# Mamba scan: two channel blocks in one scan of 1024 columns, parted by a factor of zero, with the carried state of the second block added by ScalarE

## The chip, the core and the metric

The kernel runs on one core of a Trainium2 chip. The metric is the device time of one execution in microseconds (us). Five engines have instruction queues of their own and run beside each other: TensorE (PE, with its weight loads shown as PEld), VectorE (DVE), ScalarE (ACT), GpSimd (POOL) and SyncE (SP, which only issues transfers here). Each takes its instructions in the order in which they were put into its queue; an instruction that waits holds up all that stand behind it on the same engine.

## The reference, cut to what matters

A network of four layers is computed: a Mamba layer, a dynamic convolution, linear attention with a mixture of experts, and softmax attention with a second mixture of experts. The change touches only the Mamba layer. It has two blocks (m1, m2), each over 2 images of 1024 tokens, with 512 channels and 16 states per channel:

```python
delta = softplus(dt @ dt_w + dt_b)
A = -exp(A_log)
dA = exp(delta[..., None] * A)                       # decay, per token, channel and state
dBu = delta[..., None] * Bm[:, :, None, :] * xs[..., None]
def step(hst, ins):
    dA_t, dBu_t, C_t = ins
    hst = dA_t * hst + dBu_t                         # the recurrence over tokens
    y_t = einsum('bdn,bn->bd', hst, C_t)             # sum over the 16 states
    return (hst, y_t)
h0 = zeros((b, D_INNER, D_STATE))
_, ys = scan(step, h0, ...)
y = (ys + xs * Dp) * silu(res)
```

The recurrence runs over tokens; channels and states are independent of one another. A new image starts from zero.

## The kernel before, in words

**Units.** The 2 x 1024 tokens are cut into four chunks of 512 (`TC`). A unit is one chunk of one block: m1 chunks 0 to 3, then m2 chunks 0 to 3, eight units one after the other. Chunks 0 and 2 start an image (`first`, state zero); chunks 1 and 3 take over the state that the chunk before left in `state`.

**Layout.** The 512 channels lie as four blocks (`dc`) of 128 partitions, the 512 tokens along the columns. `scan(j, ...)` loops over the 16 states `n`. For one state it does this:

1. GpSimd (L461) makes two tiles `h` of 128x1024, each for two channel blocks (`G = 2`): `du * B`. There are six buffers, three states' worth.
2. ScalarE (L468) makes for each channel block a tile `da = exp(delta * A)` of 128x512 in PSUM, out of a pool of three banks.
3. VectorE (L472) runs for each channel block a `tensor_tensor_scan` of 512 columns, `h = da * h(previous column) + h`, in place. In a first chunk it starts at 0.0; otherwise at a [128, 1] column of `state`.
4. TensorE (L440) turns `h` in `rest(n, hs)`: for each of four groups of 128 tokens four transposes, one for each channel block, fill one bank of the pool `ht` (three banks). VectorE (L449) then does `ya += ht * C`, one 128x512 instruction for each bank. For states 0 and 10 ScalarE (L447) writes the bank into `ya` or `yb` in place of that.
5. In a first chunk `keep` (L432) has ScalarE copy the last column of `h` into `state`.

**What else runs.** While a unit is scanned, the front of the next unit (projection, causal convolution, SiLU, softplus) and the back of the one before (gate, output projection, norm) are interleaved: `between` hands out their steps, `before` hands out the steps of `rest`, and both are called after each scan. These steps put matmuls into TensorE's queue, activations and table loads into ScalarE's, and elementwise work into GpSimd's. A scheduler then settles the order on each engine with costs of its own; the names of the tiles and their buffer counts decide what an instruction has to wait for. So a buffer count can move instructions that the diff does not touch.

**PSUM in this layer.** Eight banks: `m_mm` 2 (fronts, backs), `m_ht` 3, `m_da` 3. In the last unit the `m_da` pool is closed and replaced by 2 banks plus 1 bank in which the first part of the next layer's convolution is already summed up (L762).

The core of the loop before:

```python
for dc in range(NDC):
    da = self.ps_da.tile([P, TC], F32, tag="da", ...)
    nc.scalar.activation(da, delta[:, dc, :], AF.Exp, scale=self.aneg[:, i : i + 1])
    h = hs[dc // G][:, dc % G, :]
    nc.vector.tensor_tensor_scan(
        h, da, h, 0.0 if first else state[:, n, dc : dc + 1], ALU.mult, ALU.add)
    next(before, None)
    if n or dc:
        next(between, None)
```

Of the kernel before, what the change touches and what calls it, by code (L numbers as in the profile page):

```python
# [10 lines left out]
F32 = mybir.dt.float32  # L11
I32 = mybir.dt.int32
BF16 = mybir.dt.bfloat16
AF = mybir.ActivationFunctionType
ALU = mybir.AluOpType
AX = mybir.AxisListType
PSUM = bass.MemoryType.PSUM
DRAM = bass.MemoryType.DRAM

P = 128  # L20
# [7 lines left out]
TC = 512  # L28
# [3 lines left out]
NDC = DI // P  # L32
NS = 16
# [200 lines left out]
class Mamba:  # L234
# [7 lines left out]
    def __init__(self, net, m, pools, xt, x, in_w, out_w, xproj_w, dt_w):  # L242
        self.net, self.m, self.xt, self.x = net, m, xt, x
        self.wpool, self.one, self.two, self.scanp, self.dram, self.ps_mm, self.ps_da, self.ps_ht = pools
        self.weights = in_w, out_w, xproj_w, dt_w
        self.chunks = {}
        self.carry = None
# [45 lines left out]
    def front(self, j, alone=False):  # L293


        net, nc, m, one, two = self.net, self.net.nc, self.m, self.one, self.two
# [76 lines left out]
        delta = two.tile([P, NDC, TC], F32, tag="delta", name=f"{m}_delta_{j}")  # L373
# [3 lines left out]
        for dc in range(NDC):  # L377
            pool, tag = (self.ps_ht, "ht") if alone and dc else (self.ps_mm, "mm")
# [36 lines left out]
    def scan(self, j, before, between, start=False):  # L415
# [5 lines left out]
        net, nc, m, scanp = self.net, self.net.nc, self.m, self.scanp  # L421
        xs, bd, ct, delta, du = self.chunks[j]
# [4 lines left out]
        G = 2  # L427
        half = [P, G, TC]

# [25 lines left out]
        for n in range(NS):  # L455
# [9 lines left out]
            for dc in range(NDC):  # L465
                da = self.ps_da.tile([P, TC], F32, tag="da", name=f"{m}_da_{j}_{n}_{dc}")
                i = dc * NS + n
                nc.scalar.activation(  # L468
                    da, delta[:, dc, :], AF.Exp, scale=self.aneg[:, i : i + 1]
                )  # L470
                h = hs[dc // G][:, dc % G, :]
                nc.vector.tensor_tensor_scan(  # L472
                    h, da, h, 0.0 if first else state[:, n, dc : dc + 1], ALU.mult, ALU.add
                )


                next(before, None)
                if n or dc:
                    next(between, None)
# [95 lines left out]
def layer0(net, x, x_dram, m1, m2, load_image, taps, conv_dram, lg):  # L575
# [5 lines left out]
    with (  # L581
# [6 lines left out]
        tc.tile_pool(name="m_ht", bufs=3, space=PSUM) as ps_ht,  # L588
        ExitStack() as last,
    ):  # L590
        ps_da = last.enter_context(tc.tile_pool(name="m_da", bufs=3, space=PSUM))
        xt = x.rearrange("p c b t -> p c (b t)")
        pools = (wpool, one, two, scanp, dram, ps_mm, ps_da, ps_ht)
# [20 lines left out]
        for u, (m, j) in enumerate(units):  # L614
# [17 lines left out]
            else:  # L632
                last.close()
                m.ps_da = last.enter_context(tc.tile_pool(name="m_da2", bufs=2, space=PSUM))
# [1108 lines left out]
```

## Time and profile before

| what | value |
|---|---|
| time, median of 3 runs (lowest to highest) | 2189.04 us (2184.31 to 2190.55) |
| span of the profiled execution | 2186.6 us |
| first and last scan of the Mamba layer start at | 53.3 us and 1030.1 us |
| share of the span busy: PE, DVE, ACT, POOL | 87%, 64%, 44%, 47% |
| scans: 256 from zero, 256 from a carried state | 303.3 us and 318.7 us of DVE |
| accumulates of L449 (448 of them) | 320.2 us of DVE |
| exponentials of L468 (512 of them) | 349.5 us of ACT |

The profile is that of one execution. Busy time of a group of instructions is a sum over records, and the records of neighbours on one engine can overlap by some tens of ns, so that the distance from start to start is the better price of an instruction where the engine never rests. "Idle before" is the time for which an engine stood still ahead of an instruction, with the instruction that released it. The first half of the span is the Mamba layer, the second half the other layers; the share of busy time over the whole span says little of either.

### The profile page before, as it was taken

Reading aid. Unit: us, or ns where it says so; the run is one execution under the profiler, and the core shown is the slowest. Engines: PE = TensorE matmul, PEld = TensorE weight load, DVE = VectorE, ACT = ScalarE, POOL = GpSimd, SP = SyncE. Lnnn points to the kernel's source line nnn. Section 1 sums busy time; section 2 is a strip of 40 time slices with the busy share of each in tenths; the row PEclk is TensorE's granted clock in tenths of the full one; section 3 lists DMA queues with packets and bytes.
Section 4 is the critical chain, followed back from the end, with each engine's and each line's share of the span. In section 5 each row is a group of like instructions: output and inputs, shape, how many; then the busy total and the mean of one; then the engine's idle time right before and its main releaser. Section 6 shows DMA issues by size and latency. Waiting matters only on the chain.

```text
span 2186.6 us, 27311 instructions
## 1 busy us (share of the span) xinstructions
PE 1894.0 (87%) x9652; PEld 1335.5 (61%) x9652; DVE 1400.3 (64%) x2210; ACT 959.2 (44%) x1610; POOL 1028.9 (47%) x726
## 2 busy tenths in 40 slices
PE   6888898898978888788999989949999599859996
PEld 2464555556555655454646556539999467649995
DVE  6999998999999999899005475752222544432223
ACT  4676677767777767645013454411111132301111
POOL 3796787959698686965025420012332000023331
PEclk9869889898989889899999999969999799979997
DMA  2121121111212111310030100028998200059997
GB/s 106 45 68 39 37 69 35 58 35 45 62 47 60 38 49 35 85 42 17 0 64 1 48 15 10 20 82 306 326 329 323 82 10 10 20 206 327 329 323 292
DMA packets 90499, 223.87 MB, mean 102 GB/s; under 512 B 35467, under 2 KB 51728, under 8 KB 79732
## 3 DMA queue, kind: packets, MB, share of 16 engines
q1 hardware_dynamic: 77636, 198.29, 27.1%
q0 software_dynamic: 7728, 19.15, 2.9%
q10 hardware_dynamic: 4992, 4.59, 0.7%
q8 instruction: 81, 1.33, 0.3%
q14 instruction: 62, 0.51, 0.1%
HBM read 204.60 MB, written 19.37 MB: 102 GB/s over the span
## 4 chain that ended last, share of the span: by engine, by line
PE 32%; DVE 22%; issue 19%; POOL 11%; ACT 10%; DMA 5%; POOLq 0%; SPq 0%; DVEq 0%; ACTq 0%
DVE m_h L472 11%; DVE m_ya L449 6%; PE acc L762 3%; POOL x L1520 3%; POOL l_yd L1570 3%; PE m_ht L440 3%; PE early_acc L762 3%; PE av L1276 3%; ACT m_da L468 2%; PE sc L1250 2%; DMA l_yd<-y,target 2%; POOL m_h L461 2%; PE h L1099 2%; PE m_xd_ps L351 1%; PE w L1108 1%
## 5 line engine op out<-in xcount | busy, mean ns | idle before, releaser
L461 POOL TENSOR_TENSOR m_h<-m_du,m_b 128x1024 f32<-128x1024 f32 x254 | 594.5, 2364 | 196.0 <-PE m_ht L440 95.8
L440 PE MATMUL m_ht<-ident,m_h 128*128 128x128 f32 x2048 | 361.2, 305 | 119.4 <-DVE m_ya L449 83.9
L440 PEld LDWEIGHTS m_ht<-ident,m_h 128*128 128x128 f32 x2048 | 259.5, 154 | 317.8 <-DVE m_ya L449 112.7
L468 ACT ACTIVATE m_da<-m_delta,m_aneg 128x512 f32<-128x512 f32 x512 | 349.5, 690 | 220.8 <-DVE m_h L472 220.1
L1520 POOL DMA_INDIRECT x<-l_zd,source x82 | 84.8, 1034 | 573.1 <-DVE source L1465 217.1
L449 DVE SCALAR_TENSOR_TENSOR m_ya<-m_ht,m_ct,m_ya 128x512 f32<-128x512 f32 x448 | 320.2, 733 | 18.4 <-PE m_ht L440 17.5
L472 DVE TENSOR_TENSOR_SCAN m_h<-m_da,m_state,m_h 128x512 f32<-128x512 f32 x256 | 318.7, 1271 | 14.7 <-POOL m_h L461 8.7
L472 DVE TENSOR_TENSOR_SCAN m_h<-m_da,m_h 128x512 f32<-128x512 f32 x256 | 303.3, 1210 | 23.6 <-ACT m_da L468 13.1
L1550 PEld LDWEIGHTS h<-xts,we 128*128 128x128 f32 x2528 | 298.4, 194 | 7.1 <-issue 3.4
L1550 PE MATMUL h<-xts,we 128*128 128x128 f32 x2528 | 299.4, 277 | 2.2 <-issue 1.7
L1557 DVE TENSOR_TENSOR hid<-hid,h 128x512 f32<-128x512 f32 x79 | 54.3, 688 | 258.9 <-PE h L1550 258.9
L1556 ACT ACTIVATE hid<-h 128x512 f32<-128x512 f32 x79 | 47.2, 598 | 384.6 <-issue 324.0
L1564 PE MATMUL o<-we,hid 128*128 128x256 f32 x632 | 150.4, 380 | 2.2 <-DVE y L1569 1.6
L1570 POOL DMA_INDIRECT l_yd<-y,target x79 | 79.3, 1003 | 142.6 <-DVE y L1569 136.3
L1564 PEld LDWEIGHTS o<-we,hid 128*128 128x128 f32 x632 | 113.7, 190 | 15.7 <-DVE y L1569 2.8
L336 PE MATMUL m_conv<-m_pre,m_taps 128*128 128x512 f32 x240 | 114.6, 596 | 6.7 <-ACT m_gate L498 5.6
L762 PE MATMUL early_acc<-x,early 128*98 128x448 f32 (+21 forms) x308 | 97.0, 447 | 0.0
L762 PE MATMUL acc<-x,pair 128*98 128x416 f32 (+21 forms) x308 | 93.6, 452 | 0.0
L1569 DVE COPY y<-o 128x256 f32<-128x256 f32 x79 | 33.6, 425 | 69.6 <-PE o L1564 69.6
L309 PE MATMUL m_in<-x,m_in_sb 128*128 128x512 f32 x128 | 68.8, 663 | 9.8 <-ACT m_pre L313 6.9
L762 PEld LDWEIGHTS acc<-x,pair 128*98 128x98 f32 x308 | 47.7, 167 | 39.9 <-issue 34.5
L528 PE MATMUL m_out<-m_out_sb,m_xs 128*128 128x256 f32 x256 | 68.7, 397 | 0.0
(318 smaller groups left out, 2843.3 us busy)
## 6 DMA issues: line engine op xcount, KB each, us to landing
we<-in_l_experts_dram SPq DMA_DIRECT2D x82, 1536.0 KB
m_b<-m_bd SPq DMA_DIRECT2D x128, 256.0 KB
w<-in_l_w_dram SPq DMA_DIRECT2D x21, 256.0 KB
l_zd<-l_z SPq DMA_DIRECT2D x7, 512.0 KB
l_yl<-l_yd SPq DMA_DIRECT2D x10, 256.0 KB
l_yl<-l_yd ACTq DMA_DIRECT2D x10, 256.0 KB
early<-taps SPq DMA_DIRECT2D x7, 343.0 KB
pair<-taps SPq DMA_DIRECT2D x7, 343.0 KB
```

What stands on the lines that cost most here:

```text
L309: nc.tensor.matmul(ps, lhsT=self.in_sb[:, kc, mc * P : (mc + 1) * P], rhs=self.xt[:, kc, tok], start=(kc == 0), stop=(kc == NCC - 1),)
L336: nc.tensor.matmul(ps, lhsT=self.taps[:, dc * 4 + k, :], rhs=pre[:, dc, k : k + TC], start=(k == 0), stop=(k == 3),)
L440: nc.tensor.transpose(ps[:, dc * P : (dc + 1) * P], hs[dc // G][:, dc % G, i * P : (i + 1) * P], net.ident,)
L449: nc.vector.scalar_tensor_tensor(ya[:, i, :], ps, c, ya[:, i, :], ALU.mult, ALU.add)
L461: (nc.vector if start and n == 0 else nc.gpsimd).tensor_mul(h, du[:, g * G : (g + 1) * G, :], b.unsqueeze(1).to_broadcast(half))
L468: nc.scalar.activation(da, delta[:, dc, :], AF.Exp, scale=self.aneg[:, i : i + 1])
L472: nc.vector.tensor_tensor_scan(h, da, h, 0.0 if first else state[:, n, dc : dc + 1], ALU.mult, ALU.add)
L762: nc.tensor.matmul(a[:, lo - 16 * k : hi - 16 * k, co : co + n], lhsT=lhsT, rhs=self.x[:, kc, b, lo - r0 : hi - r0, ci : ci + n], start=(u ...
L1520: nc.gpsimd.indirect_dma_start(out=x, out_offset=None, in_=zd[:, :], in_offset=bass.IndirectOffsetOnAxis(ap=source[:, g : g + 1], axis=0), ...
L1550: nc.tensor.matmul(ps[:, at], lhsT=w12[:, s, kc, at], rhs=xt[:, kc * P : (kc + 1) * P], start=(kc == 0), stop=(kc == NCC - 1),)
L1564: nc.tensor.matmul(ps[:, :C], lhsT=ht[:, mc * P : (mc + 1) * P], rhs=w[:, 8 + mc, :], start=(mc == 0), stop=(mc == NHC - 1),)
L1570: nc.gpsimd.indirect_dma_start(out=yd[g], out_offset=bass.IndirectOffsetOnAxis(ap=target[:, g : g + 1], axis=0), in_=y, in_offset=None, bo ...
```

## The change

Both channel blocks of a tile `h` are scanned by one instruction of 1024 columns. So that the second block does not take over the end of the first, its first decay factor is zero: column 0 of the second half of the factor tile is set to 0.0 once at the start and never written again, since the exponential of the second half now covers columns 1 to 511 only. Where a state is carried in, the first block still gets it as the scan's starting value; for the second block ScalarE adds `state * exp(delta[0] * A)` to the first column of `h` before the scan (one [128, 1] activation for each joined scan; the factors `a0` for all 16 states come from two small exponentials in each such unit). The purpose is fewer VectorE instructions with their fixed cost: 64 scans a unit become 32.

The factor tiles are two fixed tiles of two PSUM banks each, `das[0]` for channel blocks 0 and 1 and `das[1]` for 2 and 3. They take four banks in place of three, and the bank comes from `ht`, which goes from three to two. The last unit is not joined: its scans stay at 512 columns, with three banks of `da` in place of two, and `ht` at two. In the very first front one of the four `dt` products moves from the `ht` pool to the `mm` pool.

```diff
+        joined = self.das is not None
+        if joined and not first:
+            a0 = self.one.tile([P, NDC // G, NS], F32, tag="a0", name=f"{m}_a0_{j}")
+            for g in range(NDC // G):
+                dc = g * G + 1
+                nc.scalar.activation(
+                    a0[:, g, :], self.aneg[:, dc * NS : (dc + 1) * NS], AF.Exp,
+                    scale=delta[:, dc, 0:1],
+                )
...
-            for dc in range(NDC):
-                da = self.ps_da.tile([P, TC], F32, tag="da", name=f"{m}_da_{j}_{n}_{dc}")
-                i = dc * NS + n
-                nc.scalar.activation(
-                    da, delta[:, dc, :], AF.Exp, scale=self.aneg[:, i : i + 1]
-                )
-                h = hs[dc // G][:, dc % G, :]
-                nc.vector.tensor_tensor_scan(
-                    h, da, h, 0.0 if first else state[:, n, dc : dc + 1], ALU.mult, ALU.add
-                )
...
+            for g, h in enumerate(hs):
+                da = self.das[g] if joined else None
+                for q in range(G):
+                    dc = g * G + q
+                    i = dc * NS + n
+                    if joined:
+                        a, d = da[:, q, q:], delta[:, dc, q:]
+                    else:
+                        a = self.ps_da.tile([P, TC], F32, tag="da", name=f"{m}_da_{j}_{n}_{dc}")
+                        d = delta[:, dc, :]
+                    nc.scalar.activation(a, d, AF.Exp, scale=self.aneg[:, i : i + 1])
+                    if joined and q and not first:
+                        nc.scalar.activation(
+                            h[:, q, 0:1], state[:, n, dc : dc + 1], AF.Identity,
+                            scale=a0[:, g, n : n + 1], bias=h[:, q, 0:1],
+                        )
+                    if joined and q == 0:
+                        continue
+                    dc = g * G if joined else dc
+                    hq = h.rearrange("p g t -> p (g t)") if joined else h[:, q, :]
+                    nc.vector.tensor_tensor_scan(
+                        hq, da.rearrange("p g t -> p (g t)") if joined else a, hq,
+                        0.0 if first else state[:, n, dc : dc + 1], ALU.mult, ALU.add,
+                    )
+                    for _ in range(G if joined else 1):
+                        next(before, None)
+                        if n or dc:
+                            next(between, None)
+                        dc += 1
...
-        tc.tile_pool(name="m_ht", bufs=3, space=PSUM) as ps_ht,
+        tc.tile_pool(name="m_ht", bufs=2, space=PSUM) as ps_ht,
...
-        ps_da = last.enter_context(tc.tile_pool(name="m_da", bufs=3, space=PSUM))
+        ps_da = last.enter_context(tc.tile_pool(name="m_da", bufs=1, space=PSUM))
+        das = [ps_da.tile([P, 2, TC], F32, name=f"m_da_{g}") for g in range(2)]
+        for a in das:
+            nc.vector.memset(a[:, 1, 0:1], 0.0)
...
-                m.ps_da = last.enter_context(tc.tile_pool(name="m_da2", bufs=2, space=PSUM))
+                m.das = None
+                m.ps_da = last.enter_context(tc.tile_pool(name="m_da2", bufs=3, space=PSUM))
```

## The prediction

> **What bounds the kernel now.** I read the page first: its groups by line name the costly work. The two groups of L472 are the scans that go, L449 is the accumulate that shares VectorE with them, L468 makes the factors.
>
> ```profile
> L468 ACT ACTIVATE m_da<-m_delta,m_aneg 128x512 f32<-128x512 f32 x512 | 349.5, 690 | 220.8 <-DVE m_h L472 220.1
> L449 DVE SCALAR_TENSOR_TENSOR m_ya<-m_ht,m_ct,m_ya 128x512 f32<-128x512 f32 x448 | 320.2, 733 | 18.4 <-PE m_ht L440 17.5
> L472 DVE TENSOR_TENSOR_SCAN m_h<-m_da,m_state,m_h 128x512 f32<-128x512 f32 x256 | 318.7, 1271 | 14.7 <-POOL m_h L461 8.7
> L472 DVE TENSOR_TENSOR_SCAN m_h<-m_da,m_h 128x512 f32<-128x512 f32 x256 | 303.3, 1210 | 23.6 <-ACT m_da L468 13.1
> ```
>
> ScalarE stands idle for 220 us ahead of its exponentials until a scan frees a bank; the scans wait for ScalarE and GpSimd together for only 38 us. So VectorE is the slow side. The table of stages, cut at the eight units, says the same: length of the stage, then busy time (and count) of PE, PEld, DVE, ACT, POOL.
>
> ```profile
> 292.00:419.00 127.00, 107.35 (x520) 70.72 (x519) 115.08 (x136) 93.41 (x165) 104.81 (x68) 0.91 0.18 49
> 419.00:543.00 124.00, 107.81 (x499) 70.03 (x498) 116.62 (x133) 88.16 (x130) 96.47 (x52) 0.88 0.15 48
> 914.00:1031.00 117.00, 101.18 (x499) 60.44 (x497) 114.69 (x132) 60.78 (x87) 81.76 (x39) 0.99 0.16 40
> ```
>
> VectorE is busy for 115 of 127, 117 of 124 and 115 of 117 us: it sets a unit's length. But TensorE (about 107) and GpSimd (96 to 105) are close behind, so a wait put into their queues soon shows. Next the waits by pair of engines, from the first scan to the last: total, times, longest.
>
> ```profile
> DVE m_h L472 <- POOL m_h L461: 19.2, 13, 4.9
> DVE m_h L472 <- ACT m_da L468: 19.0, 23, 2.5
> DVE m_ya L449 <- PE m_ht L440: 17.5, 26, 2.2
> ```
>
> ```profile
> PE m_ht L440 <- DVE m_ya L449: 83.9, 123, 4.1
> ```
>
> With three `ht` banks TensorE already stands 123 times before a transpose until an accumulate has freed a bank. That is the resource which the change cuts. The timeline at 314 us shows one such hand-over (start, length, instruction):
>
> ```profile
> 314.81 2.04 DVE L449 SCALAR_TENSOR_TENSOR m_ya<-m_ht,m_ct,m_ya 128x512 f32<-128x512 f32 x3
> 315.59 0.42 PEld L440 LDWEIGHTS m_ht<-ident,m_h 128*128 128x128 f32 x4 [0.95 <-DVE m_ya L449]
> 315.59 0.66 PE L440 MATMUL m_ht<-ident,m_h 128*128 128x128 f32 x4
> ```
>
> The first of the three accumulates ends at 314.81 + 0.73 = 315.54, the freed bank's transposes start 0.05 us later and take 0.66 us. With some 0.06 us for VectorE to hear of it, a bank is full again 0.77 us after it was freed; accumulates follow each other every 0.65 us ((2.04 - 0.73) / 2).
>
> **What the Trainium skill says.** "VectorE: DVE Perf Modes", section "The TRN2 errata", says that the memory latency is exposed between instructions, so that one large tile pays it once. This is what the change is after, and the trace agrees in kind: two other scans in it take 692 ns for 256 columns and 185 ns for 16, so 2.11 ns a column and some 150 ns fixed. "PSUM — Partial Sum Buffer", section "Specifications", gives eight banks of 512 fp32; pools of 2 + 3 + 3 fill them, so the fourth factor bank has to come from `ht`, as the diff does it. "ScalarE: Activation LUTs", section "What ACT_TABLE_LOAD costs", prices an activation at 186 ns + 0.833 a column, 93 ns more for each [128, 1] operand, with about 93 ns of overlap between neighbours: 705 ns for L468, measured 690.
>
> **The change, part by part.**
>
> *Scans.* Seven units are joined: 448 scans become 224. The records overlap: in the timeline at 319 us two scans from zero in a row take 2.33 us, so the second starts 2.33 - 1.21 = 1.12 us after the first, and five near 56 us take 5.67. From start to start a scan costs 0.09 us less than its record: 1.12 us from zero, 1.18 with a state. So a joined pair does not save 0.15 us: it adds 512 columns to one scan. Slopes: (1210 - 692) / 256 = 2.02 ns a column, or the 2.11 above; I take 1.06 us for 512 columns. Joined: 2.18 from zero (record 2.27), 2.24 with a state (2.33), which the first block keeps. Four units from zero have 128 joined scans and save 128 x (2.24 - 2.18) = 7.7 us; three units with a state have 96 and save 96 x (2.36 - 2.24) = 11.5 us. Sum 19 us, 15 to 25 by the two slopes. All of it is on the path, since VectorE sets the units.
>
> *The `ht` bank.* With two banks, transposes for an accumulate start only when the one two before it is done. In the changed kernel's instruction order on VectorE, of 448 accumulates 80 have exactly one accumulate between: runs of three, four or five, where scans of one state now stand side by side. The window is 0.65 us, the need 0.77: 80 x 0.12 = 10 us at least. Where TensorE's order also has front or back matmuls between the two groups of transposes (the gate's product is 1 to 3 us, two convolution taps 0.94), that comes on top unless it was done during a scan: with all of it exposed 100 windows are short by 60 us together. In the order before, with three banks, only two windows are short at all, by 0.4 us. I take 22 us: most such work stands behind a scan of 2.2 us and is hidden there; in runs of four or more it isn't. Behind a transpose that waits stand the next unit's projections and taps; ScalarE waits for those with the exponentials queued behind them.
>
> *Exponentials.* Still two of about 0.6 us for a scan, but the second waits for the first one's end, some 0.14 us, and a scan needs both. Two tiles taken in turn give about the room that three banks gave: between the end of one A scan and the next stand a B scan of 2.2 us and some accumulates, against 1.5 to 1.9 us of exponentials and add. Adds: 96 of about 0.28 us (page price 186 + 186 - 93, nearest row 298 ns for 128x4), 9 us for each of three units, where ScalarE is busy for 87 of 127 us: hidden by themselves. Not hidden is where they stand. At state 10 of a unit with a carried state ScalarE has between the adds of the two scans a table load (1.28), Ln (2.01), two identities and a copy (1.7), a table load (1.28), an exponential and the add (0.9): about 7.2 us against one scan and four accumulates, 4.8 us. Stall 2.4, where the trace of before lost 0.6 to 1.2 there. At state 5 the add of the first scan has come to stand behind a table load and SiLU: about 2 against 0.5. In four units from m1 chunk 2 on, the second exponential of a scan at state 2 stands behind the first one of state 3, which waits for the scan just ahead: 1.3 to 3.3 us. Counted like this over all scans the orders give 39 us before and 49 after; the trace measured 19.0 for the first. I add 10 us, 0 to 25.
>
> *Last unit.* 512-column scans, `ht` windows of 2.9 us: nothing. The two zero columns, six small exponentials and the moved `dt` product: nothing; they lie beside the load of x, in ScalarE's idle time, or once in the first front. GpSimd's work is the same; its tiles come free later, by less than its 20 to 30 us of slack a unit.
>
> Sum: -19 + 22 + 10 = +13 us, so 2202 us.
>
> **Rivals.** *The stalls hide behind each other* (chance 0.29): a wait for `ht` lets ScalarE catch up, the scheduler's order holds, fewer hand-overs (19.0 us of waits for ScalarE now) give some back. Then 10 - 19 - 5 = -14: 2175 us. For it: VectorE's work does fall. Against it: the 80 tight windows. *A draw* (0.13): 2189. *TensorE becomes the bound* (0.13): windows exposed in full, the front late, ScalarE late behind it: -19 + 55 + 15 = +51, 2240 us. For it: 107 us of TensorE in 124 and 84 us of waits already; against it: a busy TensorE in records is not a full one. The middle case, 2202, has 0.45.
>
> **How the numbers follow.** Slower by over 0.3%: 0.45 + 0.13 = 0.58; within 0.3%: 0.13; faster: 0.29. The range, 2168 to 2236, holds the fast rival, the draw, the middle case and most of the last one.
>
> **What would show it.** Joined scans of 2.27 and 2.33 us confirm the first step; under 2.2 would enlarge the gain. VectorE's wait for transposes in the Mamba stage should rise from 17.5 to about 40 us and its wait for ScalarE from 19 to about 29. If the first stays under 25, the `ht` step is wrong and the kernel is faster; if busy VectorE does not fall by 15 to 25 us from start to start, the scan step is.

## The result and the profile after

The changed kernel takes 2264.7 us in the median (2261.6 to 2273.7), the kernel before 2189.6 beside it: ratio 1.0355, 95% interval 1.0320 to 1.0389, some 76 us slower. The prediction was 2202 us, in a range of 2168 to 2236.

The page's groups by line. L487 is the exponential, L459 the accumulate, L497 the scan:

```profile
L487 ACT ACTIVATE m_da<-m_delta,m_aneg 128x512 f32<-128x512 f32 (+1 forms) x512 | 351.1, 688 | 167.3 <-DVE m_h L497 164.1
L459 DVE SCALAR_TENSOR_TENSOR m_ya<-m_ht,m_ct,m_ya 128x512 f32<-128x512 f32 x448 | 319.7, 736 | 65.4 <-PE m_ht L450 63.0
L497 DVE TENSOR_TENSOR_SCAN m_h<-m_da,m_h 128x1024 f32<-128x1024 f32 x128 | 291.0, 2280 | 45.9 <-POOL m_h L471 35.9
```

The same scan with a carried state, from the groups kept apart by shape (the last unit's 64 scans of 512 columns stand in a row of their own there):

```profile
L497 DVE TENSOR_TENSOR_SCAN m_h<-m_da,m_state,m_h 128x1024 f32<-128x1024 f32 x96 | 224.1, 2340 | 12.7 <-ACT m_h L489 11.8 <-ACT m_da L487 0.5
```

The scans cost what was worked out for them, 2280 and 2340 ns. What has grown is the idle time ahead of VectorE's instructions: 18.4 to 65.4 us before accumulates, 23.6 to 45.9 before scans from zero. The table of stages (length; then busy time and count of PE, PEld, DVE, ACT, POOL; then TensorE's granted clock, DMA share and GB/s) shows where:

```profile
299.00:447.30 148.30, 109.84 (x510) 71.44 (x510) 114.31 (x104) 91.87 (x164) 109.49 (x70) 0.86 0.18 49
447.30:580.30 133.00, 108.74 (x508) 69.40 (x507) 115.30 (x104) 99.25 (x164) 95.25 (x52) 0.88 0.13 40
993.30:1110.20 116.90, 102.35 (x502) 62.26 (x500) 116.46 (x133) 59.23 (x86) 79.33 (x38) 0.98 0.16 44
```

The third and fourth unit have grown from 127 and 124 to 148 and 133 us, with VectorE as busy in them as before (114 and 115 us). The last unit, which is not joined, takes 117 us as before. From the first scan to the last unit's end the kernel before took 978.0 us with VectorE busy for 919.4, the one after 1056.5 with 912.5: busy time fell by 6.9, idle time rose from 58.6 to 144.0. These 78.5 us more are the whole loss: what follows the Mamba layer takes as long as before. The waits of VectorE in that stretch, by pair (total, times, longest):

```profile
DVE m_ya L459 <- PE m_ht L450: 62.3, 76, 2.7
DVE m_h L497 <- POOL m_h L471: 36.4, 25, 5.2
DVE ln_rs L151 <- ACT ln_rs L150: 16.5, 2, 8.3
DVE m_h L497 <- ACT m_h L489: 11.8, 10, 3.2
DVE m_h L497 <- ACT m_da L487: 9.7, 7, 3.2
```

Before there were 17.5 (transposes), 19.2 (GpSimd's `h`) and 19.0 (factors). Three rows carry the growth: the wait for transposes (+45), the one for GpSimd (+17), and a new one of 16.5 us, two waits of about 8 us each, for the square root of the norm (L150). The wait for factors fell to 9.7 us, and 11.8 us for the adds came beside it. TensorE and GpSimd wait longer as well:

```profile
PE m_ht L450 <- DVE m_ya L459: 156.2, 119, 10.0
```

```profile
POOL m_h L471 <- PE m_ht L450: 120.9, 39, 7.4
POOL m_h L471 <- ACT m_da L487: 60.8, 16, 8.0
```

TensorE's wait for a freed `ht` bank went from 83.9 to 156.2 us. GpSimd's wait for transposes (a buffer of `h` is free when its transposes are done) went from 95.8 to 120.9, and the row that names ScalarE's exponentials from 1.8 to 60.8. GpSimd does not read the exponentials' results; the releaser is inferred, so that row says only that GpSimd waits longer.

The timeline from 427 us has the cause of the new row (start, length, engine and instruction, idle time before it with its releaser):

```profile
427.70 1.26 POOL L409 TENSOR_TENSOR m_delta<-m_delta,m_ln 128x512 f32<-128x512 f32 x1
...
429.00 0.31 ACT L435 ACTIVATE m_a<-m_aneg,m_delta 128x16 f32<-128x16 f32 x1 [11.89 <-POOL m_delta L409]
...
430.70 0.30 ACT L150 ACTIVATE ln_rs<-ln_mv,eps 128x4 f32<-128x4 f32 x1
...
431.03 0.18 DVE L151 RECIPROCAL ln_rs<-ln_rs 128x4 f32<-128x4 f32 x1 [8.24 <-ACT ln_rs L150]
```

One of the two small exponentials that make `a0` for the next unit (L435) was put into ScalarE's queue before GpSimd had written the `delta` that it reads. ScalarE stood for 11.9 us, with the square root and the exponentials of the running unit behind it.

The price of a joined scan from start to start also stands in the timeline, where two follow each other (x2 stands for two in a row; the length is that of both):

```profile
211.35 4.58 DVE L497 TENSOR_TENSOR_SCAN m_h<-m_da,m_state,m_h 128x1024 f32<-128x1024 f32 x2
...
308.17 4.46 DVE L497 TENSOR_TENSOR_SCAN m_h<-m_da,m_h 128x1024 f32<-128x1024 f32 x2
```

4.46 - 2.28 = 2.18 us from zero and 4.58 - 2.34 = 2.24 with a carried state; over all joined scans that are followed without a wait the median is 2.197 and 2.257. The same count in the trace of before gives 1.130 and 1.190 for 512 columns.

### The profile page after: what moved, and what is told of

Its sections match the earlier page's. It is cut to its first block, busy times and chain, and to the rows that moved or that the text cites. A ratio compares the mean times of both kernels' runs of the same rounds, so it can differ in the third digit from the quotient of the medians.

```text
span 2264.7 us, 27077 instructions
## 1 busy us (share of the span) xinstructions
PE 1898.5 (84%) x9652; PEld 1341.2 (59%) x9652; DVE 1393.4 (62%) x1988; ACT 987.0 (44%) x1712; POOL 1028.4 (45%) x726
## 4 chain that ended last, share of the span: by engine, by line
PE 23%; issue 14%; POOL 8%; DVE 8%; DMA 4%; ACT 2%; POOLq 0%; ACTq 0%; DVEq 0%; SPq 0%
POOL x L1552 3%; PE acc L794 3%; POOL l_yd L1602 3%; DVE m_h L497 3%; PE av L1308 2%; PE early_acc L794 2%; PE sc L1282 2%; DMA l_yd<-y,target 2%; PE h L1131 2%; DVE m_ya L459 2%; PE w L1140 1%; POOL band L931 1%; DMA x<-l_zd,source 1%; PE l_g L1353 1%; PE q L1254 1%
## 5 line engine op out<-in xcount | busy, mean ns | idle before, releaser
L471 POOL TENSOR_TENSOR m_h<-m_du,m_b 128x1024 f32<-128x1024 f32 x254 | 593.9, 2360 | 266.2 <-PE m_ht L450 120.9
L487 ACT ACTIVATE m_da<-m_delta,m_aneg 128x512 f32<-128x512 f32 (+1 forms) x512 | 351.1, 688 | 167.3 <-DVE m_h L497 164.1
L459 DVE SCALAR_TENSOR_TENSOR m_ya<-m_ht,m_ct,m_ya 128x512 f32<-128x512 f32 x448 | 319.7, 736 | 65.4 <-PE m_ht L450 63.0
L497 DVE TENSOR_TENSOR_SCAN m_h<-m_da,m_h 128x1024 f32<-128x1024 f32 x128 | 291.0, 2280 | 45.9 <-POOL m_h L471 35.9
L497 DVE TENSOR_TENSOR_SCAN m_h<-m_da,m_state,m_h 128x1024 f32<-128x1024 f32 (+1 forms) x160 | 304.4, 1911 | 13.2 <-ACT m_h L489 11.8
L336 PE MATMUL m_conv<-m_pre,m_taps 128*128 128x512 f32 x240 | 120.4, 625 | 0.1
L556 PE MATMUL m_out<-m_out_sb,m_xs 128*128 128x256 f32 x256 | 74.1, 414 | 0.0
```

The lines of the kernel that those rows point to most:

```text
L336: nc.tensor.matmul(ps, lhsT=self.taps[:, dc * 4 + k, :], rhs=pre[:, dc, k : k + TC], start=(k == 0), stop=(k == 3),)
L459: nc.vector.scalar_tensor_tensor(ya[:, i, :], ps, c, ya[:, i, :], ALU.mult, ALU.add)
L471: (nc.vector if start and n == 0 else nc.gpsimd).tensor_mul(h, du[:, g * G : (g + 1) * G, :], b.unsqueeze(1).to_broadcast(half))
L487: nc.scalar.activation(a, d, AF.Exp, scale=self.aneg[:, i : i + 1])
L497: nc.vector.tensor_tensor_scan(hq, da.rearrange("p g t -> p (g t)") if joined else a, hq, 0.0 if first else state[:, n, dc : dc + 1], ALU. ...
L556: nc.tensor.matmul(a, lhsT=y[:, dc, i * P : (i + 1) * P], rhs=self.out_sb[:, dc, :], start=False, stop=(dc == NDC - 1),)
```

## The experiments

Times in us; the ratio is to the kernel before in the same session, with its 95% interval. The sessions ran on different chips, so kernels of different sessions are better compared by their ratios. "Program order" means that VectorE's scans and accumulates are held in the order in which the kernel's text issues them. Some expectations call a theory by a letter: G is the adds, H the room for `h`, J the two-bank factor tile, K the copies of the state.

| kernel | time | ratio |
|---|---|---|
| before_ht2: before, two `ht` banks | 2230.7 | 1.0202 (1.0182 to 1.0222) |
| a0_late: after, `a0` made later | 2256.1 | 1.0331 (1.0308 to 1.0353) |
| no_add: after without adds and `a0` | 2259.0 | 1.0328 (1.0303 to 1.0353) |
| joined_pinned: a0_late, program order | 2223.9 | 1.0166 (1.0149 to 1.0183) |
| before_pinned: before, program order | 2188.6 | 1.0006 (0.9996 to 1.0016) |
| before_ht2_pinned: before_ht2, program order | 2206.1 | 1.0089 (1.0072 to 1.0105) |
| paired_split: two-bank tiles, scans of 512, program order | 2230.9 | 1.0199 (1.0167 to 1.0231) |
| paired_free: same order, four single banks | 2196.3 | 1.0028 (1.0017 to 1.0039) |
| before_ht2_h7: before_ht2, seventh `h` buffer | 2218.7 | 1.0137 (1.0118 to 1.0156) |
| before_ht2_pinned_h7 | 2190.9 | 1.0022 (1.0012 to 1.0033) |
| joined_pinned_h7 | 2210.2 | 1.0123 (1.0092 to 1.0155) |
| before_h7 | 2188.8 | 1.0013 (1.0004 to 1.0023) |
| before_b2: before, two `b` buffers (one run) | 2180.3 | - |
| joined_pinned_noadd | 2223.5 | 1.0187 (1.0153 to 1.0221) |
| joined_no_keep | 2222.5 | 1.0148 (1.0109 to 1.0187) |
| before_ht2_no_keep | 2216.4 | 1.0136 (1.0104 to 1.0168) |
| joined_ht3: a factor tile in SBUF, three `ht` banks | 2347.6 | 1.0752 (1.0716 to 1.0788) |
| before_ht2_da4_h7_pinned | 2174.3 | 0.9931 (0.9914 to 0.9947) |

### The bank alone, and the early `a0`

The bank is taken from the kernel before, nothing else:

```diff
-        tc.tile_pool(name="m_ht", bufs=3, space=PSUM) as ps_ht,
+        tc.tile_pool(name="m_ht", bufs=2, space=PSUM) as ps_ht,
```

> The kernel before with two transpose banks in place of three and nothing else (one PSUM bank stays unused). Theory B (the bank is the main cost): VectorE's wait for transposes in the Mamba stage rises from 17.5 to about 60 us as in the changed kernel, 2189.6 + 40 = 2230 us or more. Theory A (placing on ScalarE) and theory C (scans of 1024 columns are too coarse a hand-over): 2189.6 + 5 to 15 us, since scans of 512 columns leave the order alternating between scan and accumulate.

Measured: 2230.7 us, 45 slower. More than half of the loss needs no joined scan. VectorE's waits in it:

```profile
DVE m_h L472 <- POOL m_h L461: 57.0, 37, 5.3
DVE m_ya L449 <- PE m_ht L440: 27.6, 47, 2.7
```

The surprise is the first row. The wait for transposes, which the prediction priced, rose by only 10 us (17.5 to 27.6). The wait for GpSimd tripled, 19.2 to 57.0. Read with GpSimd's longer wait for transposes (95.8 to 122.1 us): later transposes give a buffer of `h` back later, GpSimd fills it later, and the scan that needs it stands. The seventh buffer, below, tests this.

In a0_late the changed kernel makes `a0` behind the first decay exponential of its own unit, when `delta` is there:

```diff
-            for g in range(NDC // G):              # ahead of the loop over the states
+            with net.tc.issue_after(ins):          # ins: the unit's first exponential
+                for g in range(NDC // G):
                     nc.scalar.activation(a0[:, g, :], ...)
```

> The changed kernel, with the two small exponentials for a0 put into ScalarE's queue behind the first decay exponential of the unit that uses them, in place of wherever the scheduler puts them. Theory A (a small exponential waits on ScalarE for GpSimd's delta of the next chunk and holds up everything behind it): the two waits of 11.9 us go, VectorE's two idle stretches of 8.25 us before the reciprocal go, units m1 chunk 2 and m2 chunk 0 (148 and 144 us) fall to about 137 us as m2 chunk 2 has, so 2264.7 - 20 = 2245 us. Rival B (the missing transpose bank is all): nothing to gain, since VectorE has the same runs of accumulates; 2260 us or more.

Measured: 2256.1 us, 1.0331 against 1.0355, with intervals that overlap: about 5 us, not clear of zero, and far from the 20 of theory A. The 16.5 us of waits for the square root are gone from the trace, but VectorE's waits for GpSimd have grown from 36.4 to 41.5 us and for the adds from 11.8 to 14.3. A wait of 16 us in the table was worth some 5 us.

### A third bank for the joined kernel, without taking one

To give the joined kernel its third `ht` bank, joined_ht3 puts the second factor tile into SBUF, and halves the buffers of the `b` rows to make room for it.

```diff
-        das = [ps_da.tile([P, 2, TC], F32, name=f"m_da_{g}") for g in range(2)]
+        das = [ps_da.tile([P, 2, TC], F32, name="m_da_0"), wpool.tile([P, 2, TC], F32, name="m_da_1")]
-        tc.tile_pool(name="m_ht", bufs=2, space=PSUM) as ps_ht,
+        tc.tile_pool(name="m_ht", bufs=3, space=PSUM) as ps_ht,
```

> The changed kernel with a0 placed as in a0_late and three transpose banks: one of the two factor tiles lies in SBUF in place of PSUM, and to make room the rows b have two buffers in place of four. Theory B: VectorE's wait for transposes falls to 20 us, and the kernel ends at about a0_late - 40 us, 2200 us or below; with all stalls gone 2189.6 - 17 = 2172 us. Theory C: stays within 15 us of a0_late, about 2230 us.

Measured: 2347.6 us, the slowest of all. It says nothing about the bank, because the edit brought something larger. The scans of this kernel (minimum, median, maximum in ns), and GpSimd's `h` on its page:

```profile
L500 DVE TENSOR_TENSOR_SCAN m_h<-m_da,m_h x128: 2255/2290/4490, 52.7 to 1073.2; 128x1024 f32<-128x1024 f32 x128
```

```profile
L472 POOL TENSOR_TENSOR m_h<-m_du,m_b 128x1024 f32<-128x1024 f32 x254 | 699.4, 2775 | 196.3 <-PE m_ht L451 100.9
```

Scans with both inputs in SBUF take up to 4.49 us in place of 2.28, and GpSimd's products 2775 ns on average in place of 2360. The Trainium skill, "SBUF — State Buffer", section "Who interferes with whom", says it: a VectorE instruction with two SBUF inputs contends with a GpSimd instruction that reads SBUF. The trace agrees: of the 112 joined scans with factors in SBUF 69 took over 2.45 us, while the 20 of them with no GpSimd instruction beside them took 2.35 at most. Of the 112 with factors in PSUM, which have one SBUF input, none took over 2.36. before_b2 has only the halved `b` rows:

```diff
-            b = scanp.tile([P, TC], F32, tag="b", name=f"{m}_b_{j}_{n}", bufs=4)
+            b = scanp.tile([P, TC], F32, tag="b", name=f"{m}_b_{j}_{n}", bufs=2)
```

> The kernel before with two buffers for the rows b in place of four, the side effect of joined_ht3. All theories: within 5 us of before, since a row is asked for one state (7.5 us) ahead. If it is slower, joined_ht3 has to be read with that in mind.

Measured: 2180.3 us in a single run, where before took 2185.3. The `b` rows cost nothing that this one run shows, and before_h7 below, which has them too, agrees. This side effect is also in every kernel with seven `h` buffers below.

### The order on VectorE

In the changed kernel the scheduler sets the scans of a state side by side, and accumulates in runs of up to five (53 of its 226 runs have three or more). joined_pinned holds them in program order (scan, two accumulates, scan, two accumulates), by an order between neighbours that costs no wait. before_pinned and before_ht2_pinned do the same with the other two kernels.

```diff
+        def pin(ins):
+            if last is not None:
+                net.tc.add_manual_dep(ins.ins, last.ins.name, <order only>, ...)
+            net.last = ins
-                    nc.vector.tensor_tensor_scan(...)
+                    pin(nc.vector.tensor_tensor_scan(...))
-                    nc.vector.scalar_tensor_tensor(...)
+                    pin(nc.vector.scalar_tensor_tensor(...))
```

> a0_late with VectorE's scans and accumulates kept in the order in which the program writes them (scan, two accumulates, scan, two accumulates), so that no run of three or more accumulates meets the two banks. Theory D (the scheduler's order costs the time: runs of accumulates on two banks, state adds behind other work): VectorE's wait for transposes falls from 62 to under 30 us and the time from 2256 to 2215 us or less. Theory E (two banks leave TensorE, and through it GpSimd, too little lead whatever VectorE's order is): the time stays above 2240 us and the waits change their names.

> The kernel before (three banks, scans of 512) with the same pinning: scan, accumulate in turn. Both theories: its order is nearly that already and three banks absorb the rest, so within 10 us of 2185; it is the base for the two pinned kernels with two banks. Below 2179 it would be a better version.

> The kernel before with two transpose banks and the pinned order. Theory D: the 45 us that the bank costs (2230.7) came through the order, so it falls to within 15 us of before_pinned. Theory E: the bank still costs 30 us or more against before_pinned.

Measured: joined_pinned 2223.9 us, 32 less than a0_late but 9 more than theory D asked for. VectorE's wait for transposes fell from 61.0 to 24.4 us (first line a0_late, then joined_pinned):

```profile
DVE m_ya L460 <- PE m_ht L451: 61.0, 76, 2.5
DVE m_h L510 <- POOL m_h L482: 31.0, 16, 3.7
DVE m_ya L470 <- PE m_ht L461: 24.4, 22, 8.5
```

before_pinned took 2188.6 (1.0006): with three banks the order is worth nothing. before_ht2_pinned took 2206.1, 25 less than before_ht2 and between what theories D and E asked for. So the price of the bank depends on VectorE's order: 45 us in the scheduler's, 18 in program order (1.0089 - 1.0006, times 2187). Which trait of the scheduler's order costs the 25 us is not shown. In before_ht2 only 22 of 336 runs of accumulates have three or more, fewer than the 31 of 319 in the kernel before, and what falls with the program order is the wait for GpSimd (57.0 to 20.1 us), not the one for transposes (27.6 to 26.9).

### The adds and the copies of the state

joined_pinned_noadd and no_add leave out the adds and `a0`, so that the second channel block of each pair starts from zero in units that carry a state.

```diff
-                    if joined and q and not first:
-                        nc.scalar.activation(h[:, q, 0:1], state[:, n, dc : dc + 1], AF.Identity,
-                            scale=a0[:, g, n : n + 1], bias=h[:, q, 0:1])
```

> joined_pinned without a0 and without ScalarE's state adds; it leaves out the carried state of the second channel block of each pair in units with a carried state. Theory G (the adds, each waiting for GpSimd in front of the next exponential, are what the joined scan still costs against before_ht2_pinned): the units m1 chunk 3 and m2 chunk 1 fall from 135 to under 128 us and the time from 2223.9 to 2208 us or less. Theory H (the coarser hand-over: transposes, copies of the state and GpSimd's buffers all wait for 1024 columns): within 6 us of joined_pinned, since units that start from zero, which have no adds, did not gain either.

> The changed kernel in the scheduler's own order, without a0 and the state adds (the same part is left out as in joined_pinned_noadd). Theory G: the adds and their place behind table loads cost 8 us in each of three units: 2264.7 - 5 (a0) - 24 = 2236 us or less. Theory H: 2250 us or more.

Measured: 1.0187 against 1.0166 in program order, and 1.0328 against 1.0331 (a0_late) in the scheduler's. The adds cost nothing that shows, though VectorE waits 11.8 to 18.5 us for them in the tables. Without them that time stands under other names: VectorE's wait for the factors rose from 18.7 to 31.1 us in joined_pinned_noadd, for transposes from 24.4 to 38.6. G falls.

joined_no_keep and before_ht2_no_keep leave out the copies of the last column into `state` (ScalarE, L442), so that the second chunk of each image starts from zero; ScalarE's wait before these copies had grown from 11.5 to 55.5 us after the change.

```diff
+        nc.vector.memset(self.state, 0.0)
-                if i == 0 and first:
-                    keep(n, hs)
```

> joined_pinned without ScalarE's copies of the last column into the state in units that start from zero; the carried state is left out (the state stays zero). Theory K (these copies stand in ScalarE's queue until a whole joined scan is done, 54 us of waits against 32 with scans of 512, and hold up the exponentials behind them): the units m1 chunk 2, m2 chunk 0 and m2 chunk 2 fall from 128 to 124 us or less, in all 2224 - 14 = 2210 us. Without theory K: within 5 us of 2224.

> before_ht2_pinned without the same copies (the carried state is left out in the same way), the control. Theory K: with scans of 512 they cost little, within 5 us of 2206; a fall as large as in joined_no_keep would say that the copies cost the same in both.

Measured: 1.0148 against 1.0166 for joined_pinned, intervals that overlap, where theory K asked for 14 us; and 1.0136 against 1.0089 for before_ht2_pinned, 10 us slower. K falls. Why the second became slower is open.

### A seventh buffer for `h`

If the bank acts through late buffers of `h`, one buffer more should give a part back.

```diff
-            b = scanp.tile([P, TC], F32, tag="b", name=f"{m}_b_{j}_{n}", bufs=4)
+            b = scanp.tile([P, TC], F32, tag="b", name=f"{m}_b_{j}_{n}", bufs=2)
-                h = scanp.tile(half, F32, tag="h", name=f"{m}_h_{j}_{n}_{g}", bufs=6)
+                h = scanp.tile(half, F32, tag="h", name=f"{m}_h_{j}_{n}_{g}", bufs=7)
```

> The kernel before with two transpose banks and seven buffers h in place of six (rows b with two buffers to make room, which alone cost nothing). Theory F (the missing bank acts mainly by giving back h late, so that GpSimd makes the next h late: VectorE's wait for GpSimd rose from 19 to 57 us): a seventh buffer brings 20 us or more of the 45 back, 2210 us. Theory E without that path: less than 8 us, 2223 us or more.

> joined_pinned with seven buffers h in place of six (rows b with two). Theory H: h is held for longer (a whole 1024-column scan, then two banks' worth of transposes at a time), VectorE's wait for GpSimd (31 us) halves and the time falls by 8 us or more, to 2216 us or less. Theory G: 2220 us or more.

> The kernel before with seven buffers h (rows b with two). If GpSimd's lead also limits the kernel before (VectorE waits for it 19 us), some 5 us are to be had: 2182 us. If three banks give h back in time, it is the same as before, within 3 us.

> before_ht2_pinned with seven buffers h (rows b with two), the control for joined_pinned_h7 (2210.2, 13.7 us under joined_pinned). If the seventh buffer mends what the missing bank does, it brings 8 us or more here too, 2198 us or less; if it mends what the joined scan does (theory H), nothing here, 2203 us or more.

Measured: with three banks nothing (1.0013). With two banks 12 us in the scheduler's order, between theories F and E; the wait for GpSimd fell from 57.0 us to

```profile
DVE m_h L472 <- POOL m_h L461: 35.7, 26, 6.2
```

and the one for transposes rose from 27.6 to 33.8. In program order 15 us (wait for GpSimd 20.1 to 3.3; 1.0089 to 1.0022). Joined in program order 14 by the times, 9 by the ratios (31.0 to 9.4). So in program order the seventh buffer gives back most of what the bank costs, and in the scheduler's order about a quarter. That shows the path from bank to transposes to `h` to GpSimd. The buffer brings joined scans no more than single ones, so room for `h` is not what joining costs.

### The two-bank factor tile

Program order, six buffers, two `ht` banks: single scans 2206.1, joined scans 2223.9. The joined kernel has the cheaper scans and loses 18 us more. What is left untested is the factor tile. paired_split keeps the changed kernel's two tiles of two banks and its pairs of exponentials, but scans 512 columns at a time, each from its own state:

```diff
-                    nc.vector.tensor_tensor_scan(hq, da.rearrange("p g t -> p (g t)"), hq, ...)
+                    for p in range(G):
+                        pin(nc.vector.tensor_tensor_scan(h[:, p, :], da[:, p, :], h[:, p, :],
+                            0.0 if first else state[:, n, dc + p : dc + p + 1], ALU.mult, ALU.add))
```

> joined_pinned with each joined scan cut into two scans of 512 columns again (each with its own starting state, so no a0 and no adds), on the same two factor tiles of two banks, whose two exponentials both come first. VectorE has the work of before_ht2_pinned again. Theory J (what takes the gain is the factor tile of two banks as one unit: the second exponential waits for the first, the next pair for the whole tile): this pays the tile without the gain, 2224 + 10 to 17 = 2234 to 2241 us. Theory H (what takes the gain is that a scan ends 1024 columns at a time): as before_ht2_pinned, within 6 us of 2206.

Measured: 2230.9 us, 3 short of theory J's range and far from theory H's. With scans that are no longer joined, the loss is still there: 25 us against before_ht2_pinned, and joining them takes back 7 (1.0199 to 1.0166, intervals that overlap). ScalarE in this kernel, and VectorE's scans ahead of it:

```profile
490.06 1.42 ACT L488 ACTIVATE m_da<-m_delta,m_aneg 128x512 f32<-128x512 f32 x2 [2.25 <-DVE m_h L494]
```

```profile
487.57 2.45 DVE L494 TENSOR_TENSOR_SCAN m_h<-m_da,m_state,m_h 128x512 f32<-128x512 f32 x2
```

The two scans end at 487.57 + 2.45 = 490.02 us, and ScalarE starts at 490.06. The first of them, 1.26 us long, had read its half by 488.83, and ScalarE stood idle. So it is in all 222 pairs of the trace that follow an earlier use: no first exponential starts before both scans of its tile's last use have ended. The second exponential follows the first after 1.42 - 0.69 = 0.73 us.

The tile also counts as one when it is filled. Two exponentials of one tile, and the pair of scans that needs them:

```profile
511.25 0.70 ACT L488 ACTIVATE m_da<-m_delta,m_aneg 128x512 f32<-128x512 f32 x1
...
517.20 0.69 ACT L488 ACTIVATE m_da<-m_delta,m_aneg 128x512 f32<-128x512 f32 x1
```

```profile
517.99 2.46 DVE L494 TENSOR_TENSOR_SCAN m_h<-m_da,m_state,m_h 128x512 f32<-128x512 f32 x2 [2.86 <-ACT m_da L488]
```

The first half was ready at 511.95, but its scan waited until the second exponential, behind two table loads and other work on ScalarE, had ended at 517.89. None of the 224 first scans starts before the second exponential of its tile has ended, and 25 times VectorE stands idle for that, 41.5 us in all.

But paired_split also sets two scans and two exponentials side by side. paired_free does so too, with a bank for each exponential out of a pool of four:

```diff
-                da = self.das[g]
                 for q in range(G):
+                    da = self.ps_da.tile([P, TC], F32, tag="da", ...)      # pool of four banks
-                    nc.scalar.activation(da[:, q, :], delta[:, dc, :], AF.Exp, ...)
+                    nc.scalar.activation(da, delta[:, dc, :], AF.Exp, ...)
+                    das.append(da)
```

> Before with two `ht` banks and VectorE's scans and accumulates in program order, with the pairs of paired_split (both exponentials of a pair first, then its two 512-column scans side by side, then two accumulates), but each exponential has a bank of its own out of a pool of four, which comes free when its own scan has ended. paired_split took 2230.9 us with two tiles of two banks, before_ht2_pinned 2206.1 with single banks and single scans. If the 25 us are the release of a whole two-bank tile at once (an exponential never started before both scans of the tile's last use had ended, 1.15 us after the first one's end), this kernel comes to about 2205 us, 1.009 of before, and VectorE's wait for GpSimd's h stays near 20 us as in before_ht2_pinned. If they come from setting two scans side by side and two exponentials side by side (bursts of work for TensorE and the accumulates), it stays at about 2230, 1.020, with a wait for GpSimd near 37 us. A number between splits the 25 us.

Measured: 2196.3 us, 1.0028, less than either case of the expectation. VectorE's waits in paired_split (L494) and in paired_free (L487):

```profile
DVE m_h L494 <- POOL m_h L472: 37.4, 15, 7.4
DVE m_h L494 <- ACT m_da L488: 37.2, 23, 4.2
```

```profile
DVE m_h L487 <- POOL m_h L471: 32.8, 21, 4.0
DVE m_h L487 <- ACT m_da L481: 9.3, 7, 2.0
```

The time came back in the wait for factors, not where the expectation looked for it. Here an exponential starts as soon as its own scan has ended:

```profile
471.94 0.69 ACT L481 ACTIVATE m_da<-m_delta,m_aneg 128x512 f32<-128x512 f32 x1 [2.70 <-DVE m_h L487]
```

```profile
470.64 2.45 DVE L487 TENSOR_TENSOR_SCAN m_h<-m_da,m_state,m_h 128x512 f32<-128x512 f32 x2
```

The first scan of this pair ends at about 471.90, the second at 473.09; the exponential starts at 471.94. The same four banks, the same two `ht` banks and the same pairs: as two tiles they cost 35 us more than as four (2230.9 - 2196.3; 37 by the ratios). Two smaller things differ as well: the last unit runs in pairs only in paired_free (116 us against 118), and TensorE was granted 0.89 of its clock in the Mamba layer of paired_free and 0.87 in paired_split (818 and 843 us busy); whether that follows from the waits or adds to them is open. J stands: the two-bank tile as one unit is what costs. It acts in three ways, the late release, the second exponential's wait for the first, and the first scan's wait for both; how much each weighs was not separated. An estimate from the 25 idle stretches above, each counted for no more than the 1.19 us by which one scan could have gone ahead, gives the third way 23 us at most. A joined scan could not have it otherwise: it is one instruction, which needs both banks to start and holds both until it ends.

### A version that beats both

If single banks are what the factors need, the four banks that the change gives them can be kept, with single scans, a seventh `h` buffer and program order:

```diff
-        ps_da = last.enter_context(tc.tile_pool(name="m_da", bufs=3, space=PSUM))
+        ps_da = last.enter_context(tc.tile_pool(name="m_da", bufs=4, space=PSUM))
```

(against before_ht2_pinned_h7; the last unit has three banks in place of two)

> The kernel before with the banks of the change (two `ht`, four for the factors) but single scans and single factor banks, a seventh h buffer (b rows four to two) and VectorE's scans and accumulates in program order. before_ht2_pinned_h7 with three factor banks took 2190.9 us, and VectorE waited 32 us there for ScalarE's factors and 25 us for transposes. If the fourth factor bank takes a good part of the wait for factors away, and this wait is on the path, 2175 to 2185 us, below before (0.995 to 1.0). If the 32 us are ScalarE's queue order and not the lack of a bank, or the time goes over to the wait for transposes, 2188 to 2195 us, as before.

Measured: 2174.3 us (2172.2 to 2174.4), 0.9931 of before, and 20 us less than with three factor banks (1.0022). The wait for factors with three factor banks, and then the waits with four:

```profile
DVE m_h L482 <- ACT m_da L478: 32.4, 29, 3.3
```

```profile
DVE m_ya L459 <- PE m_ht L450: 33.3, 45, 5.0
DVE m_h L482 <- ACT m_da L478: 6.1, 9, 1.5
DVE m_h L482 <- POOL m_h L471: 2.7, 3, 1.7
```

The wait for factors fell from 32.4 to 6.1 us, the one for transposes rose from 24.9 to 33.3, and most of the difference came off the total. The bank's gain is shown in this setting only, with two `ht` banks, seven buffers and program order.

## Why the prediction was wrong

The direction was forecast at 0.58, and the mechanism named first, the `ht` bank, is the largest term. The size was missed by 63 us. Two steps failed. "Two tiles taken in turn give about the room that three banks gave" put the two-bank factor tiles at nothing; they cost 35 us. And the step on the `ht` bank left out that late transposes give `h` back late, and came to 22 us in place of 45. The direction is owed to the bank alone: joining, which was forecast to gain 9 us (-19 + 10), lost 25 on top of it. With the measured terms (ratios times 2187 us):

| step of the prediction | predicted | measured |
|---|---|---|
| scans | -19 | -20 by their pitch; about -7 of it reached the total (program order, not clear of zero) |
| `ht` bank | +22 | +45 in the scheduler's order, +18 in program order |
| factor tiles of two banks | 0 | +25 against single scans and banks, +35 to +37 with the tiles changed and single scans kept |
| adds and order on ScalarE | +10 | the adds 0; the order alone not measured |
| six small exponentials | 0 | about +5, not clear of zero |
| sum | +13 | +76 in the scheduler's order |

**Scans: right.** Records of 2.28 and 2.34 us (2.27 and 2.33 were forecast). By the median pitches of both traces 128 x (2 x 1.130 - 2.197) + 96 x (2 x 1.190 - 2.257) = 20 us were saved, inside the 15 to 25. VectorE's busy time fell by only 6.9 us, though. Counted without overlaps, the scans gave 17 us less and the accumulates 8 more: of 448 accumulates 325 are now followed without a wait, 390 before, and where a wait comes between, the overlap of some 0.09 us is lost.

**`ht` bank: right mechanism, wrong size, half the path.** VectorE's wait for transposes should have gone from 17.5 to about 40 us and went to 62.3. The step's floor of 80 x 0.12 us was even a little high, since VectorE starts 0.04 us after the last transpose in the trace of before, not 0.06 (median of 33). What the step left out is that transposes release `h`. "GpSimd's work is the same; its tiles come free later, by less than its 20 to 30 us of slack a unit" was the sentence that failed: slack summed over a unit does not help a scan that needs one buffer now. In before_ht2 the wait for GpSimd grew by 38 us, the one for transposes by 10.

**"Two tiles taken in turn give about the room that three banks gave": wrong.** The step compared two lengths, an average, and found room. paired_split against paired_free puts it at 35 us. It is the step whose failure is worst, as it was costed at nothing without a count of what is queued on ScalarE between two releases or between the two exponentials of one scan.

**Adds: +10 was wrong.** VectorE's wait for ScalarE's factors and adds was forecast to go from 19 to about 29 us and went to 21.5 (9.7 + 11.8), and taking the adds away gives nothing. The prediction added stalls that lie side by side with others.

**"The six small exponentials: nothing": wrong.** Their work is nothing. Their place in ScalarE's queue is 11.9 us of waiting, twice. Little of it reached the total; where the rest went is seen only in the waits of a0_late that grew.

**Do the terms add up?** In the scheduler's order: bank +45, joining with late `a0` +25 (2256.1 - 2230.7), early `a0` about +5, together 75. The forecast had 22, -9 and 0 for these, so of the 63 us missed the bank has 23, joining 34 and `a0` 5. In program order: bank 18, joining 18. Of the joining term in the scheduler's order only the sum is measured; that it is made of the tile and the scans in the same shares as in program order is not shown.

**The rivals.** "TensorE becomes the bound" came nearest with 2240 us, but not by its mechanism: TensorE is busy for 837 us of the 1056, 833 of the 978 before. It does not work more, it waits more. Nor is its clock the loss: it was granted 0.87 of it in this stretch and 0.89 before, and the busy time shows 4 us of that. The range, which was said to hold most of this rival, ended 4 us below its 2240. "The stalls hide behind each other" (2175 us) did happen in part, with the adds and most of the early `a0`, but the two large terms did not hide.

## What to carry to other kernels

Merging two instructions also merges the buffers that they read: a buffer of two banks is given back at the end of the longer instruction, so the producer loses the time in which it used to refill the first half, and the longer instruction starts only when both halves are full. Before taking a buffer away, follow who refills what once it is free, through all engines, and ask what the order of instructions makes of it: the same bank cost 18 us in program order and 45 in the scheduler's. And a row in the table of waits is not a price: waits of 12 and 16 us here were worth 0 and about 5, one that fell by 26 was worth 20, and one that fell by 28 went with 35.

## What had not been expected of the hardware

A scan of 1024 columns with factors in PSUM takes 2.28 us beside a busy GpSimd; with factors in SBUF up to 4.49, and GpSimd's product of 128x1024 up from 2.36 us to a mean of 2.78. Without GpSimd beside it, the scan with factors in SBUF took no more than 2.35. Moving a factor tile out of PSUM is no way to gain a bank here.

An activation on a single column with two [128, 1] operands (L489) takes 381 ns on average (36.5 us for 96). The Trainium skill, "ScalarE: Activation LUTs", section "What ACT_TABLE_LOAD costs", has prices from which 186 + 2 x 93 + 0.8 = 373 is an estimate; the trace agrees within 2%.

Two exponentials in a row into the two halves of one tile start 0.72 us apart (median of 104 in paired_split), into separate banks 0.62 (median of 80 in paired_free). The wait for a neighbour on the same engine thus takes away the overlap, 0.1 us each time.
